# A sparse GAT kernel: empty list entries skipped by the gathers, their factor columns cleared on GpSimd, and two batches instead of one scaled on ScalarE

## The chip, the cores and the metric

The kernel runs on one core of one Trainium2 chip. The metric is the device time of one execution in microseconds (us); the number given for a kernel is the median of its runs. All data is float32 except where the code says otherwise.

## The reference

The input `x` is 8 batches x 2048 nodes x 128 features; `adj` is a 2048 x 2048 matrix of zeros and ones in which about 1 entry in 128 is set. Four graph layers follow each other: two attention layers with 8 heads and a small feed-forward network (layers 0 and 1), and two GAT layers (layers 2 and 3). The change is in the GAT layers. Each of them computes, cut to what matters:

```python
h = x @ W
s_i = h @ a_src
s_j = h @ a_dst
e = s_i[:, :, None] + s_j[:, None, :]
e = jnp.where(e >= 0, e, NEG_SLOPE * e)
e = jnp.where(adj[None, :, :] == 0, -jnp.inf, e)
att = jax.nn.softmax(e, axis=-1)
out = jnp.einsum('bij,bjd->bid', att, h)
y = out + x        # then a layer norm with ln_gamma, ln_beta
```

So each node takes a weighted mean over its neighbours' rows `h`. The weight of a neighbour is the exponential of a leaky relu of a sum of two numbers, one of the node and one of the neighbour.

## The kernel before

**Lists.** The kernel treats the graph as sparse. It sorts the 2048 nodes by degree into 16 blocks `t` of 128 nodes, one node per partition, and makes for each block a list of neighbour numbers of fixed length `CAPS[t]` (30 for the first block, 11 for the last; in the first, the last two list columns, called folded, hold the surplus of its 16 largest nodes). The lists of all blocks have 277 columns together. A node with fewer neighbours than its block's list has empty entries; they hold the number N = 2048, one past the last node.

**Tables and gathers.** For each layer `l` a table in DRAM has one row per node. In the attention layers a row is 8192 bytes (keys and values of 8 batches); in the GAT layers it is 4160 bytes: `h` of the 8 batches (8 x 128 numbers), and then 16 factors, two for each batch, which are the exponentials of the neighbour's number and of 0.2 times that number. `gather` (L319) issues one indirect DMA per list column on GpSimd's queue: it brings 128 rows, one into each partition. An entry over its `bounds_check` is skipped. In the attention layers entries over N - 1 are skipped. In the GAT layers the table has one row more, row N, which is all zeros, and entries up to N are fetched.

**Chunks.** In the GAT layers a chunk is up to 4 list columns of one block; there are 75 chunks in a layer. `fetch` takes the next of six buffers `kv` (`KVB = 6`) and issues the chunk's gathers, a few chunks ahead of the one in work. Each gather waits until TensorE has used up the old contents of its part of the buffer. `gat_chunk` then does, for a chunk:

- on VectorE, L785 multiplies the second factor of each batch by the node's own number, L786 takes the larger of the two factors (the weight, kept in `pair` in PSUM), and L791 does so once more for the last `SCALED` batches, into the small tile `ws` in SBUF;
- L797 on VectorE multiplies the rows of the first `8 - SCALED` batches by their weights; L802 on ScalarE multiplies those of the last `SCALED` batches, one instruction per list column and batch;
- in layer 2 alone, L808 on VectorE adds the rows of the chunk's last list column to those of its first;
- `add_up` (L326) on TensorE transposes and adds the chunk's rows into the accumulator `acc`, one matmul with the identity per list column and batch.

After a block's last chunk come its sums (L471 to L478), `outputs` (L678) and `gat_tail`: residual and layer norm on TensorE (L836) and ScalarE (L844, L852), a transpose (L859), and in layer 2 the projection for the next layer's table (L548, L557, L562 to L568), whose rows GpSimd scatters to DRAM (L515). In layer 3, L882 and L884 apply the norm's gain and offset and GpSimd scatters the block to the output (L886). SyncE loads and stores the blocks' states, one load per block and layer and one store.

**Order.** The order on each engine is the order in which the Python code emits the instructions, written out by hand in `layers` with generators: for chunk i it emits the weights and products of chunk i, then the pair sum and the adding up of chunk i - 1, and in between calls `slot`, which advances the tails by a step and lets `fetch` run. So on VectorE the L808 of a chunk comes after the L797 of the next, and on GpSimd gathers and scatters stand in one row.

A layer's first gathers can start once most rows of its table have been written; the lists of the first two blocks are sorted so that their first chunks need only the rows of early blocks.

Of the kernel before, what the change touches and what calls it, by code (L numbers as in the profile page):

```python
# [8 lines left out]
F32 = mybir.dt.float32  # L9
# [9 lines left out]
B, N, D = 8, 2048, 128  # L19
# [9 lines left out]
NB = 8  # L29
# [1 line left out]
LN_EXP = 6  # L31
KVB = 6
STATES = 4
SCALED = 1

# [47 lines left out]
def sparse_path(ctx: ExitStack, tc: tile.TileContext, ins: dict, out: bass.AP, flag: bass.AP):  # L85
# [10 lines left out]
    nc = tc.nc  # L96
# [3 lines left out]
    dram = ctx.enter_context(tc.tile_pool(name="dram", bufs=1, space=bass.MemoryType.DRAM))  # L100
# [39 lines left out]
    bufs = [const.tile([P, CHUNK], F32, name=f"kv{i}") for i in range(KVB)]  # L140
    turn = [-1]

    def buffer():
        turn[0] += 1
        return bufs[turn[0] % KVB]
# [155 lines left out]
    def width(l):  # L301
        return NB * (2 * D if l < 2 else D + 2)


    tables = [dram.tile([N + (l > 1), width(l)], F32, name=f"table{l}") for l in range(4)]

    x_rows = ins["x_nodes"]

# [9 lines left out]
    def gather(l, index, dst):  # L318
        nc.gpsimd.indirect_dma_start(  # L319
            out=dst, out_offset=None, in_=tables[l][:, :],  # L320
            in_offset=bass.IndirectOffsetOnAxis(ap=index, axis=0),
            bounds_check=N - (l < 2), oob_is_err=False,
        )

    def turn_into(dst, src, start):
        nc.tensor.matmul(  # L326
            dst, src, ident, start=start, stop=True, is_transpose=True, skip_group_check=True
        )
# [439 lines left out]
    def gat_chunk(l, c):  # L768
# [18 lines left out]
        if c["folded"]:  # L787
            box["wf"] = small.tile([P, FOLD, NB], F32, tag="wf", name="wf", bufs=1)
            nc.vector.tensor_max(box["wf"], wa, wb)
        ws = small.tile([P, 4, SCALED], F32, tag="ws", name="ws", bufs=3)  # L790
        nc.vector.tensor_max(  # L791
            ws[:, :ns, :], wa[:, :, NB - SCALED :], wb[:, :, NB - SCALED :]
        )
        yield
        hv = hs[:, :, : NB * D].rearrange("p s (b c) -> p s b c", b=NB)
        nv = NB - SCALED
        nc.vector.tensor_mul(  # L797
# [96 lines left out]
    def start():  # L894
# [173 lines left out]
        next(weights, None)  # L1068
        for i in (3, 4, 5):
            nc.scalar.copy(bufs[i], nil.to_broadcast([P, CHUNK]))  # L1070
        for l in (2, 3):
            nc.sync.dma_start(tables[l][N : N + 1, :], bufs[5][:1, : width(l)])


    def verdict():
# [29 lines left out]
    for l in range(4):  # L1105
        per = 2 if l < 2 else 4
        for t, k, ns, folded in pieces(l, per):
            c = dict(l=l, t=t, k=k, ns=ns, folded=folded, box=blocks[l][t])
# [11 lines left out]
    def fetch():  # L1120

        while now[1] < len(every):
            c = every[now[1]]
            l, t, k, ns = c["l"], c["t"], c["k"], c["ns"]

            if now[1] - now[0] > (4 if now[1] >= KVB and every[now[1] - KVB]["l"] > 1 else 3):
                return
            resorted = l > 0 and t < 2 and not c["folded"]
            need = NT - max([b for end, b in EARLY[t] if k + ns <= end] + [0] if resorted else [0])
            if put[l] < need:  # L1130
                return
            c["buf"] = buffer()[:, : ns * width(l)].rearrange("p (s c) -> p s c", s=ns)
            for i in range(ns):
                at = t * BASE if resorted else first[t]
                index = (sorted_lists if resorted else lists)[:, at + k + i : at + k + i + 1]
                gather(l, index, c["buf"][:, i])
            now[1] += 1
# [6 lines left out]
    def slot():  # L1144
        advance(threads)
        advance(tails)
        fetch()
        beat[0] += 1
        if beat[0] % 3 == 0 and hurry():
            advance(tails)  # L1150
# [40 lines left out]
    def layers():  # L1191
        threads.append(first_states((0,)))
        drain()
        fetch()
        begin(every[0])
        for _ in weights:
# [4 lines left out]
        for i in range(len(every) + 2):  # L1201
            c1, c, n1, n2 = (chunk(i + j) for j in range(-1, 3))
            while added:
                c2 = added.pop(0)
                go(c2)
                if c2["last"]:
                    threads.append(tail(c2["l"], c2["t"], c2["box"]))
            now[0] = i
            fetch()
            if c["k"] == 0:  # L1210
                l, t = c["l"], c["t"]
# [44 lines left out]
    with tc.manual_schedule():  # L1256
        nc.scalar.add_instruction(
            mybir.InstLoadActFuncSet(name=nc.get_next_instruction_name(), act_func_set_id=LN_EXP)
        )
        start()  # L1260
        layers()
# [521 lines left out]
```

## Time and profile before

| What | Value |
|---|---|
| Median of 3 runs | 3161.54 us (3149.05 to 3168.80) |
| Profiled execution, its own time | 3022.89 us |
| Span of the profiled execution | 3021.1 us |
| TensorE busy | 2517.4 us (83%) |
| TensorE weight loads busy | 2320.8 us (77%) |
| VectorE busy | 2743.3 us (91%) |
| ScalarE busy | 1379.7 us (46%) |
| GpSimd busy | 1784.3 us (59%) |
| Mean granted TensorE clock | 0.939 |
| Moved by DMA | 987.63 MB, mean 327 GB/s |

The page of the profile gives for each group of instructions its line, engine, operation, tiles (out<-in), count, busy time in us, mean duration in ns, and the idle time of its engine just before it with what ended that idle time. PE is TensorE, PEld its weight loads, DVE VectorE, ACT ScalarE, POOL GpSimd, SP SyncE. A table of stretches gives the busy time of each engine between two times, the granted clock, the mean busy share of the 16 DMA engines (values a little over 1 occur) and what they moved. The profiled execution is one of its own; the runs for the median were others.

### The profile page before, as it was taken

To read this page: it belongs to the slowest core of one execution; us is meant where nothing else is said; L and a number is where in the kernel's file an instruction comes from. 1 tells how busy PE (TensorE), PEld (TensorE's weight loads), DVE (VectorE), ACT (ScalarE), POOL (GpSimd) and SP (SyncE) were. 2 spreads that over 40 slices of the span, in tenths; PEclk is the share of its full clock that TensorE was granted. 3 is DMA by queue.
4 is the path that set the end of the run, shared out by engine and by line. 5 is a ranking of instruction groups with operands and counts; after the bars stand their busy time and mean duration, and the time that the engine had idled before them with its cause. 6 is when DMAs were issued, how large, how long until landed. Compare 5 with 4: busy or idle time off the path is not lost.

```text
span 3021.1 us, 52130 instructions
## 1 busy us (share of the span) xinstructions
PE 2517.4 (83%) x19258; PEld 2320.8 (77%) x19258; DVE 2743.3 (91%) x2945; ACT 1379.7 (46%) x4898; POOL 1784.3 (59%) x1293
## 2 busy tenths in 40 slices
PE   5756888789889999688888898999678898788886
PEld 3646777778788898677888788888578888687786
DVE  8788999999999998999999999998599998499996
ACT  4721333444445555043444454545345556244454
POOL 0057578677755644545546555554577775477773
PEclk8978999999999999899999999999798899899998
DMA  8688889988988887778888889886799999799995
GB/s 331 234 301 320 310 310 324 347 299 314 362 304 335 313 305 316 279 260 343 307 322 325 344 323 333 322 309 241 259 395 403 397 414 355 261 411 412 409 412 216
DMA packets 200692, 987.63 MB, mean 327 GB/s; under 512 B 31918, under 2 KB 33712, under 8 KB 128436
## 3 DMA queue, kind: packets, MB, share of 16 engines
q0 software_dynamic: 175024, 890.45, 77.7%
q1 hardware_dynamic: 20502, 75.52, 6.5%
q10 hardware_dynamic: 4904, 18.24, 1.9%
q8 instruction: 155, 2.54, 0.3%
q14 instruction: 107, 0.88, 0.1%
HBM read 937.16 MB, written 91.55 MB: 341 GB/s over the span
## 4 chain that ended last, share of the span: by engine, by line
PE 36%; DVE 30%; DMA 16%; issue 9%; ACT 5%; POOL 1%; POOLq 0%; DVEq 0%; ACTq 0%
PE acc L326 12%; DMA kv<-table,lists 11%; DVE kv L640 9%; DVE kv L659 8%; PE pair L648 5%; DVE kv L645 4%; DMA kv<-table,sorted_lists 3%; PE m L752 3%; DVE kv L797 3%; PE m L731 2%; PE m L533 2%; PE m L333 2%; DMA table<-rows,perm 2%; PE m L557 1%; PE m L548 1%
## 5 line engine op out<-in xcount | busy, mean ns | idle before, releaser
L319 POOL DMA_INDIRECT kv<-table,lists x955 | 1334.0, 1397 | 764.8 <-PE acc L326 491.9
L326 PE MATMUL acc<-ident,kv 128*128 128x128 f32 x8208 | 1059.8, 285 | 180.0 <-DVE kv L659 98.4
L326 PEld LDWEIGHTS acc<-ident,kv 128*128 128x128 f32 x8208 | 978.2, 148 | 258.7 <-DVE kv L659 120.5
L640 DVE TENSOR_TENSOR kv<-kv,q 128x2048 f32<-128x2048 f32 (+1 forms) x282 | 629.2, 2231 | 46.5 <-DMA kv<-table,lists 18.7
L659 DVE TENSOR_TENSOR kv<-kv,w 128x2048 f32<-128x2048 f32 (+1 forms) x284 | 632.4, 2227 | 0.0
L648 PE MATMUL pair<-kv,ident 128*128 128x128 f32 (+1 forms) x3344 | 444.3, 284 | 141.5 <-issue 66.7
L797 DVE TENSOR_TENSOR kv<-kv,pair 128x3584 f32<-128x3584 f32 (+1 forms) x150 | 540.0, 3600 | 1.9
L648 PEld LDWEIGHTS pair<-kv,ident 128*128 128x128 f32 x3344 | 411.7, 197 | 167.1 <-issue 100.3
L653 ACT ACTIVATE w<-pair,lmask 128x64 f32<-128x64 f32 x554 | 144.7, 311 | 738.8 <-PE pair L648 738.7
L645 DVE TENSOR_TENSOR kv<-kv 128x1024 f32<-128x1024 f32 (+1 forms) x434 | 442.5, 1020 | 14.3
L494 ACT ACTIVATE n<-m,eps 128x128 f32<-128x128 f32 x512 | 181.5, 367 | 296.8 <-PE m L718 154.3
L319 POOL DMA_INDIRECT kv<-table,sorted_lists x153 | 188.4, 1231 | 126.3 <-PE acc L326 56.6
L802 ACT ACTIVATE kv<-kv,ws 128x128 f32<-128x128 f32 x554 | 177.9, 400 | 180.6 <-DVE ws L791 173.9
L844 ACT ACTIVATE n<-m,eps 128x128 f32<-128x128 f32 x256 | 90.8, 374 | 183.1 <-PE m L836 183.1
L515 POOL DMA_INDIRECT table<-rows,perm x57 | 85.1, 1493 | 132.9 <-ACT score L568 31.4
L752 PE MATMUL m<-w_L_w,hT 128*128 128x128 f32 x1024 | 156.2, 275 | 0.0
L501 ACT ACTIVATE n<-m,rs 128x128 f32<-128x128 f32 x512 | 146.3, 376 | 1.1
L752 PEld LDWEIGHTS m<-w_L_w,hT 128*128 128x128 f32 x1024 | 134.9, 192 | 0.0
L731 PE MATMUL m<-n1T,w_L_gnn_W 128*128 128x512 f32 x256 | 131.5, 597 | 0.6 <-ACT q L606 0.6
L333 PE MATMUL m<-ident,n 128*128 128x128 f32 x640 | 107.8, 291 | 11.9 <-ACT rows L562 7.5
L678 DVE TENSOR_TENSOR o<-acc,scale 128x512 f32<-128x512 f32 x128 | 82.9, 683 | 37.6 <-PE acc L326 23.3
L333 PEld LDWEIGHTS m<-ident,n 128*128 128x128 f32 x640 | 83.4, 151 | 36.2 <-issue 14.7
(238 smaller groups left out, 3615.4 us busy)
## 6 DMA issues: line engine op xcount, KB each, us to landing
kept<-xT SPq DMA_DIRECT2D x48, 512.0 KB, 6.2
xT<-kept SPq DMA_DIRECT2D x48, 512.0 KB, 7.5
kv<-in_adj_dram SPq DMA_DIRECT2D x16, 1024.0 KB, 6.5
table<-kv ACTq DMA_DIRECT2D x16, 1024.0 KB, 5.7
kv<-table,lists POOLq DMA_INDIRECT x955, 8.6
kv<-in_x_nodes_dram SPq DMA_DIRECT2D x16, 512.0 KB, 12.5
kv<-table,sorted_lists POOLq DMA_INDIRECT x153, 6.9
found<-cand POOLq DMA_DIRECT2D x16, 64.0 KB, 4.3
```

Source lines behind the costliest of these rows:

```text
L319: nc.gpsimd.indirect_dma_start(out=dst, out_offset=None, in_=tables[l][:, :], in_offset=bass.IndirectOffsetOnAxis(ap=index, axis=0), bound ...
L326: nc.tensor.matmul(dst, src, ident, start=start, stop=True, is_transpose=True, skip_group_check=True)
L333: nc.tensor.transpose(pt[:, j * P : (j + 1) * P], src[:, j, :], ident)
L494: nc.scalar.activation(dst[:, i, :], z[:, i, :], AF.Square, bias=eps, scale=D**-0.5, accum_out=ss[:, i : i + 1],)
L640: nc.vector.tensor_mul(kk, kk, q[:, None].to_broadcast([P, ns, NB, D]))
L645: nc.vector.tensor_add(kk[:, :, :, :width], kk[:, :, :, :width], kk[:, :, :, width : 2 * width])
L648: nc.tensor.matmul(sc, ident, kk[:, :, :, j : j + NH], start=j == 0, stop=j + NH == width)
L659: nc.vector.tensor_mul(vv, vv, w[:, k : k + ns, :].rearrange("p s (b h) -> p (s b) h", h=NH)[:, :, None, :] .to_broadcast([P, ns * NB, HD, ...
L731: nc.tensor.matmul(ph, wt["1"][:, f * P : (f + 1) * P], n1T.rearrange("p b c -> p (b c)"), start=True, stop=True,)
L752: nc.tensor.matmul(y[:, j, :], hT[:, f, j, :], wt["2"][:, f, :], start=False, stop=f == 1, skip_group_check=True,)
L797: nc.vector.tensor_mul(hv[:, :, :nv, :], hv[:, :, :nv, :], wc[:, :, :nv, None].to_broadcast([P, ns, nv, D]))
L802: nc.scalar.mul(hv[:, i, b, :], hv[:, i, b, :], ws[:, i, b - nv : b - nv + 1])
```

## The change

Three edits, all for the GAT layers:

- The tables lose their row of zeros, and the gathers of every layer skip entries over N - 1, so an empty entry leaves the old contents of its partition in the buffer.
- So that such an entry counts for nothing, `fetch` clears the 16 factor columns of all of the chunk's list columns with one GpSimd memset ahead of the chunk's gathers (128 partitions x up to 4 x 16 numbers); the weight of an entry that isn't fetched is then zero. The two loads of zero rows at the end of `start` go.
- `SCALED` goes from 1 to 2: L797 covers six batches instead of seven, L802 two instead of one, and `ws` is twice as wide.

```diff
-SCALED = 1
+SCALED = 2
...
-    tables = [dram.tile([N + (l > 1), width(l)], F32, name=f"table{l}") for l in range(4)]
+    tables = [dram.tile([N, width(l)], F32, name=f"table{l}") for l in range(4)]
...
         nc.gpsimd.indirect_dma_start(
             out=dst, out_offset=None, in_=tables[l][:, :],
             in_offset=bass.IndirectOffsetOnAxis(ap=index, axis=0),
-            bounds_check=N - (l < 2), oob_is_err=False,
+            bounds_check=N - 1, oob_is_err=False,
         )
...
-        for l in (2, 3):
-            nc.sync.dma_start(tables[l][N : N + 1, :], bufs[5][:1, : width(l)])
...
             c["buf"] = buffer()[:, : ns * width(l)].rearrange("p (s c) -> p s c", s=ns)
+            if l > 1:
+                nc.gpsimd.memset(c["buf"][:, :, NB * D :], 0.0)
             for i in range(ns):
```

In the changed kernel's order on GpSimd each memset stands directly ahead of its chunk's first gather, and that gather waits for the memset's semaphore besides those it waited for before.

## The prediction

> **What bounds the kernel now.** I read the page first, then the table of stretches, then the lines of GpSimd and VectorE in those stretches, and last the order of time on GpSimd alone. The change touches only the two GAT layers, so the averages over the span say little. From the starts of the score product (L785) the GAT layers run from 2078 us on; layer 3's first gather is issued at 2546 us and the last scatter at 3015 us. Each layer has 277 gathers of 128 rows in 75 chunks. I cut out the two steady parts, and the two parts in which a layer starts:
>
> ```profile
> core 0: us, PE busy (x) PEld busy (x) DVE busy (x) ACT busy (x) POOL busy (x), PEclk, DMA share, GB/s
> 2170.00:2525.00 355.00, 299.52 (x2297) 284.05 (x2297) 340.48 (x394) 190.84 (x761) 263.76 (x241) 0.90 1.01 397
> 2637.00:2975.00 338.00, 284.13 (x2331) 273.94 (x2330) 310.03 (x372) 164.09 (x638) 254.57 (x249) 0.93 1.02 410
> ...
> 2060.00:2170.00 110.00, 85.10 (x646) 76.58 (x645) 68.53 (x68) 54.03 (x209) 50.77 (x45) 0.89 0.65 228
> 2525.00:2637.00 112.00, 86.85 (x668) 83.62 (x668) 63.95 (x74) 47.02 (x191) 53.62 (x53) 0.85 0.76 286
> ```
>
> In both steady parts the DMA engines are full (1.01 and 1.02). VectorE is nearly full in layer 2 (340 of 355) and at 310 of 338 in layer 3. GpSimd seems to have a quarter free, but its busy time hides a fixed gap. The order of time on GpSimd, at the start of layer 3 where few transfers are under way:
>
> ```profile
> 2628.70 0.99 POOL L319 DMA_INDIRECT kv<-table,sorted_lists  x1 [0.30 <-issue]
> 2629.99 0.99 POOL L319 DMA_INDIRECT kv<-table,sorted_lists  x1 [0.30 <-DMA kv<-table,sorted_lists]
> 2631.29 0.99 POOL L319 DMA_INDIRECT kv<-table,sorted_lists  x1 [0.30 <-DMA kv<-table,sorted_lists]
> ```
>
> A gather is 0.99 us and then always 0.305 us until the next: 1.295 us at best. The previous transfer of the same lane had landed some 4 us earlier, so it isn't the DMA that sets this. GpSimd's floor in a stretch is its instructions times 1.295: 241 x 1.295 = 312 of 355 us in layer 2 and 248 x 1.295 = 321 of 338 us in layer 3. A gather also costs the DMA engines about the same: its 128 packets of 4160 bytes take 161 ns each by the median, eight on each of 16 engines, 1.29 us. So two resources stand at their limit side by side, and VectorE is a third in layer 2:
>
> ```profile
> L797 DVE TENSOR_TENSOR kv<-kv,pair 128x3584 f32<-128x3584 f32 (+1 forms) x63 | 226.2, 3590 | 0.9
> L808 DVE TENSOR_TENSOR kv<-kv 128x1024 f32<-128x1024 f32 x62 | 75.5, 1218 | 7.7 <-ACT kv L802 7.7
> L802 ACT ACTIVATE kv<-kv,ws 128x128 f32<-128x128 f32 x224 | 72.1, 401 | 25.0 <-DVE ws L791 18.2 <-issue 6.7
> L844 ACT ACTIVATE n<-m,eps 128x128 f32<-128x128 f32 x104 | 36.9, 375 | 96.3 <-PE m L836 96.3
> L902 POOL MEMSET kv<- x3: 141/141/141, 3.1 to 3.3; 128x64 f32 x3
> ```
>
> The reader should see that L797 is two thirds of VectorE's time, that ScalarE mostly waits for TensorE, and that a memset of 64 elements per partition is 141 ns.
>
> [...] for a layer-1 gather with 63 rows filled, eight of the 16 completions came within 1.8 us and the other eight 3.4 to 4.9 us after the first. [...] L802 lasts 401 ns, but four in a row take 1.28 us, 0.32 us each.
>
> **The change part by part.**
>
> Skipped entries. The inputs give 32733 edges for 277 x 128 = 35456 list slots, so 2723 entries (7.7%) per layer are empty. Layers 0 and 1 already skip: their gathers' 8192-byte packets number 65466 = 2 x 32733, so a skipped row moves nothing. The GAT layers now save 2 x 2723 packets. But nodes are sorted by degree within a block, so the empty rows lie in the high partitions. [...] With about 165 ns a packet that is 227 gathers x 1.32 x 0.044 = 13 us off layer 2's steady 355 us (floor 342), and 235 x 1.32 x 0.044 = 14 us off layer 3's 338 (floor 324). GpSimd's issue doesn't shrink: gathers with 96 or more empty entries in layers 0 and 1 have the same 0.99 us at their fastest.
>
> Memsets on GpSimd. 75 per layer, 62 and 64 in the steady parts. The built order puts each ahead of its chunk's gathers, and the first gather then also waits for the memset's semaphore. Behind it stand the chunk's other gathers, the row scatters (L515) or output scatters (L886) and the next chunks. Each memset breaks the 1.295 us rhythm by M = (end of the last gather to memset) + 0.14 + (memset's semaphore to gather) - 0.305. A gather held by TensorE's semaphore starts 0.259 us after it, over and over in the trace; a compute instruction behind another on GpSimd starts at once (the three memsets above start 0.08 us apart), but none stands behind a gather. Low end: 0 + 0.14 + 0.26 - 0.305 = 0.1 us. If the memset also has to sit out the 0.305: 0.4 us. High end: the semaphore counts like the landing of an old transfer, 0.745 us before the start: 0.05 + 0.14 + 0.745 - 0.305 = 0.63 us. A gain from it is excluded, since nothing is taken from GpSimd. I take 0.2 us, because the built program puts the memset's semaphore on the gather itself, as TensorE's is[...].
>
> One more batch on ScalarE. L797 goes from 3584 to 3072 elements; its two forms (3886 ns for 3584, 2953 for 2688) give 1.04 ns an element, so 0.53 us for a chunk of four, 0.49 on the mean: 62 x 0.49 = 30 us off VectorE in each steady part, 310 of 355 and 280 of 338 remain. ScalarE gets 224 more multiplications at 0.32 us, 72 us: 263 and about 239. The waits for TensorE (96 us in layer 2 alone) cover them; in a burst of tail work, where ScalarE is busy 12 us on end and TensorE waits for it, they would lengthen the burst by up to 4 us a block. VectorE's pair sum (L808) of a chunk comes after the next chunk's L797, so ScalarE has a chunk's time to finish.
>
> The two loads of a zero row on SyncE's queue at 162 us were 4 KB each with nothing behind them: nothing.
>
> Sum against the profiled execution's 3022.9 us (span 3021.1). Layer 2: DMA 342, GpSimd 312 + 62 x 0.2 = 324, VectorE 310, TensorE 300; with 2 us of friction (my guess) 344, that is 11 us less. Layer 3: DMA 324, GpSimd 321 + 64 x 0.2 = 334, plus 2: 336, that is 2 us less; here GpSimd takes over from the DMA engines. The two starts have 24 of the 150 chunks, some of whose memsets are on the way: 2 us more; ScalarE's longer bursts: 2 us more. Together 9 us less, 0.30%. The runs' median of 3161.5 us lies 139 us above the profiled execution, for a reason that the profile doesn't show; I carry the share over: 3161.5 x 0.9970 = 3152.
>
> **The rivals.**
>
> Slower: the hand-over on GpSimd costs 0.63 us. Layer 3 becomes 321 + 64 x 0.63 + 2 = 363, 25 more; layer 2 312 + 39 + 2 = 353, 2 less; the starts 8 more, ScalarE 2 more. 33 us more, 1.1%: 3196. It speaks for it that GpSimd is already at 95% of its floor in layer 3 and that every chunk passes through it; against it the 0.259 us after TensorE's semaphore. The point from which it decides is M = 0.4 us: there 64 x 0.4 - 15 = 11 us lost in layer 3 meet layer 2's gain.
>
> Faster: the memset fits the gap (M = 0.05) and the packets, now fewer, also lose their stretch from 161 to 165 ns. Layer 2: 21 less, layer 3: 14 less (GpSimd's floor 324 holds it there): 35 us, 3125. Against it: it needs both.
>
> ScalarE's bursts eat layer 2's gain: TensorE waits 10 us there for L859 already. Layer 2 unchanged, the rest as forecast, and its gain of 11 gone: 2 us more, 3164, within 1%.
>
> The change doesn't do what it says: skipped rows still cost their packets. Then only the memsets' price is left, about 13 us in layer 3 and 2 in the starts: 3177. The count in layers 0 and 1 speaks against it.
>
> **How the numbers follow.** Forecast 0.5; slower rival 0.2; faster 0.12; ScalarE 0.15; no skip 0.03. A change of 1% (32 us) is about what a measurement of this kernel can tell from none. The forecast's own spread (M of 0.1 to 0.4) gives 3144 to 3169. The range takes in the faster rival's and the slower one's centre, and some scatter between runs: 3118 to 3200. Faster by over 1%: 0.12 and a little of the forecast, 0.15. Slower by over 1%: the slower rival and a little of ScalarE's case, 0.23. Within: 0.62.
>
> **What would show it.** Right: packets of 4160 bytes fall from 75776 to 70330; the gap from a chunk's last gather to the next chunk's first is about 0.5 us with a memset in it, against 0.305; the DMA share falls below 1.0 in layer 3 while GpSimd's gathers stand in an unbroken row; VectorE's L797 is near 3.1 us; layer 2 shrinks more than layer 3. Wrong: a gap of 0.9 us or more around each memset, ScalarE as the releaser of TensorE's L326 or VectorE's L808 in most chunks, or a DMA share still at 1.02.

## The result, and the profile after

The change made the kernel slightly slower: 3183.9 us (median of 7 runs, 3162.88 to 3189.59) against 3164.42 us (3149.05 to 3174.81), a ratio of 1.0058 with a 95% interval of 1.0032 to 1.0084. A second set of runs (e8, on the chip called B below) gave 1.0104 (1.0077 to 1.013). The forecast was a small gain, 9 us; by the medians the loss is 19 us in the first set and 26 us in the second, whose ratio makes it 33 us.

One thing is needed before the profiles can be read. The runs of this study were made on several chips of the type, and they are not alike. On four of them the kernel before takes 3146 to 3161 us at a mean granted clock of 0.921 to 0.922; on the fifth it takes 3031.66 us at 0.939. The profiled execution on which the prediction was worked out (3022.89 us, clock 0.939) looks like the fifth; the timed runs look like the other four, and all experiments but e17 and e18 come from them. Each chip was used for one series of runs, so whether the chip itself makes the difference, or something about that series, isn't shown. I call the chips A to E; the table gives the kernel before on each.

| Chip | Experiments | Kernel before, median | Mean clock |
|---|---|---|---|
| A | e1 to e4 | 3147.71 us | 0.922 |
| B | e5 to e8 | 3150.17 us | 0.921 |
| C | e9c to e12c | 3160.86 us | 0.921 |
| D | e13 to e16 | 3146.25 us | 0.921 |
| E | e17, e18 | 3031.66 us | 0.939 |

So the profile after must be set beside a profile of the kernel before from an ordinary chip (e1, chip A, span 3143.4 us), not beside the first one. Table of stretches, the change (first gather of layer 2 at 2070 us, of layer 3 at 2620 us, span 3161.1 us):

```profile
2170.00:2600.00 430.00, 330.83 (x2302) 306.26 (x2302) 316.30 (x399) 251.97 (x971) 282.85 (x317) 0.81 0.88 317
2700.00:3100.00 400.00, 309.52 (x2253) 280.82 (x2251) 275.72 (x364) 219.09 (x829) 268.34 (x319) 0.87 0.92 329
```

The same stretches of the kernel before on chip A (layer 3 from 2611 us):

```profile
2170.00:2600.00 430.00, 337.00 (x2367) 314.56 (x2367) 352.66 (x407) 198.00 (x779) 281.71 (x258) 0.83 0.94 350
2700.00:3100.00 400.00, 319.06 (x2370) 293.78 (x2370) 315.32 (x375) 165.54 (x651) 259.16 (x252) 0.87 0.96 357
```

The columns are those of the prediction: TensorE, its weight loads, VectorE, ScalarE and GpSimd busy, then clock, DMA share and GB/s. Already before the change nothing is as full here as in the first profile: DMA 0.94 and 0.96 in place of 1.01 and 1.02, VectorE 353 of 430 us, TensorE at a clock of 0.83. The change takes load from VectorE (353 to 316) and from the DMA engines, puts 54 us on ScalarE in each stretch, and TensorE gets fewer matmuls done in the same time (2302 for 2367). The groups on the page after show that each edit did what it says:

```profile
L797 DVE TENSOR_TENSOR kv<-kv,pair 128x3072 f32<-128x3072 f32 (+1 forms) x150 | 466.3, 3108 | 1.7
...
L802 ACT ACTIVATE kv<-kv,ws 128x128 f32<-128x128 f32 x1108 | 337.3, 400 | 53.7 <-DVE ws L791 22.4
...
L808 DVE TENSOR_TENSOR kv<-kv 128x1024 f32<-128x1024 f32 x75 | 91.7, 1223 | 98.4 <-ACT kv L802 78.0
```

L797 fell from 540.0 us on the page before to 466.3, 0.49 us a chunk, and L802 nearly doubled, from 177.9 to 337.3. The last line has the new wait: VectorE stood idle 78 us before its pair sum, until ScalarE's product was done; in the stretch of layer 2 shown with the prediction that was 7.7 us. In the waits of layer 2 (2170 to 2600 us; us in total, times, longest), the change:

```profile
DVE kv L808 <- ACT kv L802: 68.6, 20, 9.7
...
POOL kv L319 <- PE acc L326: 58.5, 19, 8.3
```

and the kernel before on chip A:

```profile
POOL kv L319 <- PE acc L326: 69.6, 29, 8.0
...
DVE kv L808 <- ACT kv L802: 45.8, 13, 8.9
```

On chip A the kernel before already had 45.8 us of this wait. A sign of what a batch on ScalarE costs could be seen there, but not in the profile that I had.

### The profile page after: what moved, and what is told of

Its sections match the earlier page's. It is cut to its first block, busy times and chain, and to the rows that moved or that the text cites. A ratio compares the mean times of both kernels' runs of the same rounds, so it can differ in the third digit from the quotient of the medians.

```text
span 3161.1 us, 52991 instructions
## 1 busy us (share of the span) xinstructions
PE 2585.7 (82%) x19258; PEld 2358.4 (75%) x19258; DVE 2673.6 (85%) x2945; ACT 1537.2 (49%) x5452; POOL 1778.9 (56%) x1443
## 2 busy tenths in 40 slices
DMA packets 200694, 965.03 MB, mean 305 GB/s; under 512 B 37362, under 2 KB 39156, under 8 KB 128432
## 4 chain that ended last, share of the span: by engine, by line
PE 42%; DVE 24%; issue 10%; DMA 9%; ACT 8%; POOL 3%; another core or an unknown queue 1%; POOLq 0%; ACTq 0%; DVEq 0%
PE acc L326 17%; DVE kv L640 8%; DVE kv L659 8%; DMA kv<-table,lists 7%; PE pair L648 5%; DVE kv L645 4%; PE m L731 2%; PE m L752 2%; POOL kv L319 2%; ACT kv L802 2%; ACT n L844 2%; PE m L333 2%; PE m L533 2%; PE m L836 2%; PE m L557 2%
## 5 line engine op out<-in xcount | busy, mean ns | idle before, releaser
L326 PE MATMUL acc<-ident,kv 128*128 128x128 f32 x8208 | 1089.1, 287 | 212.6 <-DVE kv L659 95.2
L326 PEld LDWEIGHTS acc<-ident,kv 128*128 128x128 f32 x8208 | 988.9, 149 | 309.7 <-issue 147.1
L797 DVE TENSOR_TENSOR kv<-kv,pair 128x3072 f32<-128x3072 f32 (+1 forms) x150 | 466.3, 3108 | 1.7
L802 ACT ACTIVATE kv<-kv,ws 128x128 f32<-128x128 f32 x1108 | 337.3, 400 | 53.7 <-DVE ws L791 22.4
L844 ACT ACTIVATE n<-m,eps 128x128 f32<-128x128 f32 x256 | 90.5, 369 | 251.2 <-PE acc L326 150.0
L808 DVE TENSOR_TENSOR kv<-kv 128x1024 f32<-128x1024 f32 x75 | 91.7, 1223 | 98.4 <-ACT kv L802 78.0
L333 PE MATMUL m<-ident,n 128*128 128x128 f32 x640 | 116.4, 304 | 24.1 <-ACT kv L802 8.9
```

Source lines behind the costliest of these rows:

```text
L326: nc.tensor.matmul(dst, src, ident, start=start, stop=True, is_transpose=True, skip_group_check=True)
L333: nc.tensor.transpose(pt[:, j * P : (j + 1) * P], src[:, j, :], ident)
L797: nc.vector.tensor_mul(hv[:, :, :nv, :], hv[:, :, :nv, :], wc[:, :, :nv, None].to_broadcast([P, ns, nv, D]))
L802: nc.scalar.mul(hv[:, i, b, :], hv[:, i, b, :], ws[:, i, b - nv : b - nv + 1])
```

## The experiments

The first eight ask which edit costs the time, the next four why ScalarE's batch costs it and what sets layer 3, the last six why fewer packets gave nothing. Ratios are to the kernel before on the same chip, with 95% intervals; microseconds given for an experiment are its ratio's distance from 1 times the median of before on that chip.

**e1, the kernel before again.** No edit.

> The kernel before, unchanged, for a second profile of it. If the profiled execution of 3022.9 us was unusual (theory U), this profile shows a span near 3150 us, with the GAT layers 100 us or more longer than the 944 us of the first profile and gaps in TensorE's rows that wait for nothing shown. If the profile is usual and only the timed runs are longer (rival), the span is again near 3020 us and the GAT layers near 944 us.

1.0016 (0.9998 to 1.0033). Its profile (3143.4 us) isn't like the first one. Layers 0 and 1 last the same in both, 950 us each; the GAT layers last 539 and 533 us instead of 480 and 475.

**e2, skipping and memset, one batch on ScalarE.** The change with `SCALED = 1`.

> The changed kernel with SCALED back at 1: skipped entries and memsets alone. Theory S (the second batch on ScalarE is what costs: the pair sum and TensorE's adding up wait for it): faster than before by 5 to 20 us, 3145 to 3160. Theory G (the memset in GpSimd's row costs more than the skipped packets give): slower than before by 5 to 20 us, and about as slow as the whole change, 3170 to 3185.

0.9999 (0.9975 to 1.0022). Two of the three edits together move nothing beyond the interval, some 8 us either way. Neither theory had foreseen that.

**e3, two batches alone.**

```diff
-SCALED = 1
+SCALED = 2
```

> The kernel before with SCALED at 2 alone: row N still fetched, no memsets. Theory S: slower than before by 20 to 40 us, 3185 to 3205, with L808 and TensorE waiting for L802 as in the profile after. Theory G: no slower than before, 3150 to 3165, since VectorE loses 0.5 us a chunk.

1.0125 (1.008 to 1.0169): the whole loss is here.

**e4, the memset alone.** The memset in `fetch`, on rows that are all fetched.

> The kernel before with the memset ahead of each GAT chunk's gathers added, nothing else: row N still fetched, SCALED 1. It measures the memset by itself. By the profile after, a memset adds 0.14 us to GpSimd's row, 150 times, 21 us at most. Theory S: 0 to 15 us slower than before. Theory G: 20 us slower or more.

1.0001 (0.9981 to 1.0021). 150 memsets on GpSimd cost nothing beyond the interval, some 7 us either way.

**e5 and e6, two batches in one layer.**

```diff
-SCALED = 1
+SCALED_OF = {2: 2, 3: 1}
...
+        SCALED = SCALED_OF[l]
```

(e6: `{2: 1, 3: 2}`.)

> The kernel before with two batches on ScalarE in layer 2 alone (layer 3 keeps one; no skipping, no memsets). Theory S1 (the loss is layer 2's, where VectorE's pair sum L808 waits for ScalarE's products): 25 to 45 us slower than before, as much as two batches in both layers (38 us). Theory S2 (ScalarE's longer row delays the tails in both layers): about half of that, 15 to 22 us slower.

> The kernel before with two batches on ScalarE in layer 3 alone, which has no pair sum. Theory S1: within 8 us of before, on either side. Theory S2: 15 to 22 us slower.

e5 1.0078 (1.0054 to 1.0102), e6 1.0005 (0.998 to 1.003). Within these intervals the loss is in layer 2 alone, 24.6 us at chip B's level. Nor does VectorE's relief of half a microsecond a chunk gain anything in layer 3 that they show.

**e7, VectorE's pair sum without ScalarE's batches.** `SCALED = 2`, but L808 adds only the six batches that VectorE multiplied, and TensorE adds the other two of the last column itself, so L808 waits for no one.

```diff
-            nc.vector.tensor_add(hv[:, :pairs], hv[:, :pairs], hv[:, left:ns])
+            nc.vector.tensor_add(hv[:, :pairs, :nv], hv[:, :pairs, :nv], hv[:, left:ns, :nv])
...
+        for i in range(left, ns):
+            for b in range(nv, NB):
...
+                    turn_into(acc[:, b, :], hv[:, i, b, :], False)
```

> Two batches on ScalarE in both layers, no skipping, no memsets; layer 2's pair sum on VectorE covers only the six batches that VectorE scaled itself, and TensorE adds the other two batches of the last list column with two matmuls of its own (0.2 us a chunk). Theory S1: the loss of 38 us goes; within 10 us of before. Theory S2, or TensorE's own wait for ScalarE as the cause: still 25 us slower or more.

1.0134 (1.01 to 1.0168), against 1.0104 for the change on the same chip. The most visible new wait, L808's, is gone (0.0 us of idle time before L808), and the loss stays. But VectorE now waits elsewhere in layer 2 (2170 to 2650 us):

```profile
DVE o L678 <- PE acc L326: 72.5, 8, 11.3
DVE o L678 <- ACT kv L802: 41.8, 4, 14.4
DVE ws L791 <- ACT kv L802: 19.2, 12, 2.9
```

In e3 the first two of these were 9.0 and 5.3 us, and the third isn't among VectorE's waits there. The edit also gives TensorE two matmuls more a chunk: in the steady part of layer 2, from the 51st gather to the last, it was busy 361 us, against 336 in e3. So e7 shows that taking this one wait away gains nothing; it doesn't show that the wait is harmless.

**e8, the change again.**

> The changed kernel once more, beside the others on the same chip. If skipping gives back part of what the second batch costs, it is 15 to 25 us slower than before, and some 15 to 20 us faster than two batches alone (38 us slower). If the two only differed by chance between chips, it is 30 to 40 us slower.

1.0104 (1.0077 to 1.013), 33 us. That speaks for chance between chips as the difference between the change and e3; the interval, 24 to 41 us, leaves room for a small part given back by skipping.

**e9c, less TensorE work in layer 3.** Two of the eight batches of every list column but a block's first are not added up (522 of 2216 matmuls left out).

```diff
...
-            for b in range(NB):
+            for b in range(NB - (less if k + i > 0 else 0)):
...
```

> The kernel before, in whose layer 3 TensorE leaves out two of the eight batches' adding up in every list column but a block's first (522 of the layer's 2216 such matmuls; those two batches of the output are then not sums). Everything else stays. Theory P (in the ordinary executions TensorE alone sets layer 3's time, so that fewer packets, memsets and VectorE's 0.5 us a chunk count for nothing there): 45 to 80 us faster than before. Rival (the gathers set it, by DMA or by GpSimd's rhythm): less than 10 us faster.

0.9984 (0.9966 to 1.0001): 5 us, at most 11, though TensorE is, just ahead of VectorE, the busiest engine of that layer (319 and 315 of 400 us in e1's table). Theory P falls.

**e10c, idle work on ScalarE.** One batch on ScalarE as before; in layer 2 each list column gets one more multiplication (277 in all) from constants into a tile that nobody reads.

```diff
...
+        for i in range(ns if l == 2 else 0):
+            nc.scalar.mul(idle, ident, node[:, i : i + 1])
```

> The kernel before with, in layer 2, one more multiplication of 128x128 on ScalarE per list column, behind L802, on a tile that nobody reads: 277 x 0.32 = 89 us of ScalarE's row and nothing that another engine waits for. Theory O (what the second batch costs is room in ScalarE's row: the tails' steps behind it come late, and TensorE waits for them in order): 20 to 40 us slower. Theory D (the cost is that TensorE and the pair sum wait for the second batch's products): within 8 us of before.

1.0046 (1.0023 to 1.0068), 14.5 us. Nothing waits for this work's result, VectorE isn't relieved, and no transfer changes; only the place in ScalarE's row is taken. It costs more than half of the 24.6 us of the real second batch. Behind this work the one real batch comes later too: the pair sum's wait for it in layer 2 is 70.5 us, against 45.8 in e1. So e10c shows that the place costs, and not which of ScalarE's late results does the harm.

**e11c, no batch on ScalarE in layer 2.** VectorE multiplies all eight there; L791 and L802 go from layer 2.

```diff
-SCALED = 1
+SCALED_OF = {2: 0, 3: 1}
...
+        if SCALED > 0:
...
```

> The kernel before with no batch on ScalarE in layer 2 (L797 covers all eight there; layer 3 keeps one). Theory O: the mirror image of the loss as long as VectorE has room, 10 to 25 us faster. If VectorE's row becomes layer 2's bound (0.5 us more a chunk on 321 of 380 us): slower by up to 15 us.

0.9935 (0.9918 to 0.9951), 3139.03 against 3160.86 us: faster than both kernels. VectorE is fuller in this version's layer 2 than in e1's:

```profile
2170.00:2600.00 430.00, 336.17 (x2424) 312.85 (x2425) 386.69 (x353) 133.80 (x563) 292.65 (x262) 0.84 0.96 357
```

VectorE is busy 387 of 430 us (353 in e1), and still more gets done than before (2424 matmuls in the stretch for 2367, 262 instructions on GpSimd for 258).

**e12c, layer 3's pair sum moved to VectorE.** Two batches on ScalarE in layer 3 (one in layer 2), and L808 in every second chunk of it, which takes matmuls from TensorE.

```diff
...
-        pairs = min(ns // 2, 1) if l == 2 else 0
+        pairs = min(ns // 2, 1) if l == 2 or k // 4 % 2 == 0 else 0
```

> A version that follows from theory P: one batch on ScalarE in layer 2 and two in layer 3, and layer 3 also adds a chunk's last list column to its first on VectorE, in every other chunk (41 of 75), which takes 41 x 8 matmuls off TensorE and puts 41 x 1.2 us on VectorE. Theory P: 25 to 45 us faster than before. Rival: no faster than before.

1.0048 (1.0029 to 1.0066): the room that the second batch gives on VectorE in layer 3 can't be turned into time this way.

**e13, three quarters of the rows in layer 3.** On e2's version (which is level with before):

```diff
-            bounds_check=N - 1, oob_is_err=False,
+            bounds_check=(3 * N // 4 if l == 3 else N) - 1, oob_is_err=False,
```

> Skipping and memset with one batch on ScalarE, and in layer 3 the gathers also skip every node number of 1536 and over: a quarter of the neighbours are left out, 25% of layer 3's packets go, and every instruction on GpSimd, VectorE, ScalarE and TensorE stays. Without the last edit this version measured 0.9999. Theory D (the DMA engines, with their slow packets, set layer 3 in ordinary executions): a quarter of some 316 us of packet time goes, and the layer shrinks until the next row decides (GpSimd's gathers at 320 us of 381): 30 to 60 us faster, 0.98 to 0.99. Theory G (GpSimd's own issue row): within 5 us, since every gather is still issued. Theory T (TensorE with its throttle, or a pause that no other engine ends): within 5 us.

0.997 (0.9948 to 0.9991), 9 us. Three times as many further packets as the change skips (25% of 32733 against 2723) give less than a third of the least that theory D asked. The at most 5 us of theories G and T lie within the interval. The stretch in layer 3:

```profile
2700.00:3000.00 300.00, 236.59 (x1736) 217.53 (x1736) 229.74 (x270) 115.19 (x450) 199.41 (x237) 0.86 0.77 259
```

The DMA share is down to 0.77 and the stretch holds no more work for it: e2 has 1714 matmuls and 236 instructions on GpSimd in its 2700 to 3000 us, at a DMA share of 0.92.

**e14, fewer gathers in layer 3.** On e2's version, the last column of each chunk of three or four isn't gathered.

```diff
-            for i in range(ns):
+            for i in range(ns - (l == 3 and ns > 2)):
```

> Skipping and memset with one batch on ScalarE, and in layer 3 the last list column of each chunk of three or four is not gathered at all (74 of 277 gathers; its factors are cleared by the memset, so a part of the neighbours is left out); the work on VectorE, ScalarE and TensorE stays. Both GpSimd's row (74 x 1.295 = 96 us) and the packets (about 27%) fall. Theory D: like the kernel with three quarters of the rows, 0.98 to 0.99. Theory G: 30 to 60 us faster, 0.98 to 0.99, while the kernel with three quarters of the rows stays within 5 us. Theory T: within 5 us, as the other.

0.9705 (0.9672 to 0.9738), 93 us. Layer 3 lasts 448 us instead of some 530, and VectorE becomes its bound:

```profile
2690.00:2990.00 300.00, 266.00 (x2229) 255.43 (x2228) 286.93 (x342) 155.53 (x608) 189.25 (x234) 0.95 0.93 327
```

That is the direction of theory G, though it had asked for 30 to 60 us only; but the clock in that stretch also rose to 0.95 from 0.84 (e2, same stretch), and the columns that are not gathered reach TensorE as zeros, so the gain could come from what TensorE is given. e17 and e18 are for that.

**e15, no batch on ScalarE in either layer.** e11c with `{2: 0, 3: 0}`.

> The kernel before with no batch on ScalarE in either GAT layer: VectorE multiplies all eight batches, L791 and L802 go. In layer 2 alone this measured 0.9935. In layer 3 a second batch moved nothing (1.0005). If ScalarE's row costs nothing in layer 3 and VectorE has room (it was busy 303 of 380 us in an ordinary execution; 64 more products of 0.5 us make 335), the result is that of layer 2 alone, 0.993 to 0.995. If VectorE becomes layer 3's bound with its load, 10 to 20 us are lost again: 0.997 to 1.000.

0.9892 (0.9858 to 0.9926), 3118.96 against 3146.25 us: better than I expected of it, and the fastest version here that computes all of the reference. VectorE has the room in layer 3. Whether the layer gains by it too isn't settled: e11c's interval, on chip C, overlaps with this one.

**e16, no batch in layer 2, with skipping and memset.**

> No batch on ScalarE in layer 2, one in layer 3, with the change's skipping and memset. If the packets that are skipped cost nothing there even when ScalarE is out of the way, the result is that of no batch in layer 2 alone, 0.993 to 0.994. If ScalarE's row had hidden the gain of fewer packets in layer 2, a part of the 13 us reckoned for it shows now: 0.989 to 0.992.

0.9922 (0.9896 to 0.9948), in agreement with e11c's 0.9935. So ScalarE hadn't hidden a gain of the skipped packets: even with its row free in layer 2 they give none that the intervals show.

**e17 and e18, issues and zeros told apart, on chip E.** e17: e14's columns are gathered, but with a bound that skips their rows (issue kept, packets gone, zeros kept). e18: as e14, and TensorE adds the chunk's first column a second time in place of the last (issue gone, packets gone, no zeros).

```diff
...
+                gather(l, index, c["buf"][:, i], 0 if l == 3 and ns > 2 and i == ns - 1 else N - 1)
```

```diff
...
-                    turn_into(acc[:, b, :], rows[:, i, b, :], k + i == 0 and b % 4 == 0)
+                    turn_into(acc[:, b, :], rows[:, 0 if again and i == n - 1 else i, b, :], k + i == 0 and b % 4 == 0)
```

> As the kernel with fewer gathers in layer 3 (0.9705), but the last column's gather of each chunk of three or four is issued and then skips its rows (all but those of node 0; these neighbours are left out again). GpSimd's row is whole again, while the packets stay about 27% fewer and TensorE still gets zeros for 74 columns. Theory G (GpSimd's issue row: 74 x 1.295 = 96 us): the gain is gone, 0.99 to 1.00. Theory Z (the gain came from the zeros, which TensorE does at a less throttled clock: it was 0.96 there against 0.88): 0.97 to 0.975, as without the issue.

> As the kernel with fewer gathers in layer 3 (0.9705), but TensorE adds the chunk's first column a second time in place of the last, which is not gathered: the matmuls are as many and none of them is of a column of zeros; VectorE and ScalarE do what they did (the last column's neighbours are left out and the first's count twice). Theory G: the gain stays, 0.97 to 0.975. Theory Z: the gain goes, 0.99 to 1.00. If a part goes, both have a share.

e17 0.9951 (0.9934 to 0.9969), e18 0.9863 (0.9842 to 0.9883): 15 and 42 us against the kernel before; their layers 3 last 462 and 440 us, 475 in the first profile. (e2's version wasn't run on chip E, so skipping and memset have a share in both that isn't known.) Table of stretches, e17:

```profile
2637.00:2975.00 338.00, 287.36 (x2388) 277.07 (x2385) 312.41 (x368) 170.36 (x669) 257.02 (x305) 0.94 0.89 300
```

and e18:

```profile
2645.00:2945.00 300.00, 264.96 (x2246) 256.60 (x2245) 295.42 (x355) 159.17 (x625) 189.48 (x234) 0.95 0.91 331
```

e17 can be laid beside the first profile of before, over the same stretch: the DMA share is down from 1.02 to 0.89, and the gathers from the 51st to the last take the same 325 us. GpSimd's row accounts for it: 237 gathers and scatters at 1.295 us and 61 memsets at 0.14 make 315 of these 325 us. Without the issues (e18) the layer shortens until VectorE is full, 295 of 300 us. So on chip E theory G holds for the larger part of the gain, 27 of 42 us, and zeros don't explain it: e18 has none. For the rest of e14's 93 us on chip D they can't be excluded, since what chip D loses there isn't lost on chip E to begin with (see the pauses below).

## Why the prediction was right or wrong

**Right: what the edits do.** The bytes moved fell from 987.63 to 965.03 MB, and the packets of 4160 bytes from 75778 to 70330: 2 x 2723 rows and the two loads of zero rows. Before:

```profile
DMA packets 200692, 987.63 MB, mean 327 GB/s; under 512 B 31918, under 2 KB 33712, under 8 KB 128436
```

After:

```profile
DMA packets 200694, 965.03 MB, mean 305 GB/s; under 512 B 37362, under 2 KB 39156, under 8 KB 128432
```

The number of packets didn't fall: 5444 became small ones. In the trace a skipped row is a packet of 4 bytes that takes 9 ns; "moves nothing" was right enough. L797's new mean is 3.11 us, as reckoned.

**Right: the price of a memset, M.** In order of time on GpSimd, the change, layer 3 (start, us, line, and idle time before it):

```profile
2841.59 1.02 POOL L886 DMA_INDIRECT out_dram<-n,perm  x1 [0.30 <-issue]
2842.62 0.17 POOL L1133 MEMSET kv<- 128x64 f32 x1
2843.06 1.02 POOL L319 DMA_INDIRECT kv<-table,lists  x1 [0.27 <-issue]
```

From the scatter's end at 2842.61 to the gather at 2843.06 are 0.44 to 0.45 us where 0.305 stood: M = 0.14 us, taken as 0.2 with 0.1 to 0.4 as its range. Of the 150 hand-overs in this profile 93 take less than 0.5 us, 0.44 by the median. The memset starts at once (0.00 us after the instruction ahead of it, by the median of the 93), the gather 0.27 us after it, as a gather after TensorE's semaphore does (0.26). A memset beside VectorE's pair sum takes no longer in this profile: the 13 that ran beside an L808 took 0.16 to 0.18 us, the 137 others 0.14 to 0.18, both 0.166 by the median. The slower rival (0.63) is out. Even this small price doesn't show in the runs (e4).

**Wrong: ScalarE's second batch, 2 us.** This is the term that failed. The prediction set 72 us of new work against 96 us in which ScalarE waited for TensorE, allowed up to 4 us more per block in a burst, and then put down 2 us in all. Its own upper end, 4 us for each of the 13 blocks of the steady part (104 L844, eight a block), is 52 us; the measured cost is 25 us (e5). Two of its reasons failed as well. "ScalarE has a chunk's time to finish" did not hold: L808 waited 78 us for L802. And TensorE's wait for L859 was not 10 but 20 us already in the first profile: 10.4 before L548, which is the prediction's 10, and 9.2 before L326.

ScalarE's free time isn't where its work is. In e1 ScalarE is busy 198 of 430 us of layer 2, and still the 277 multiplications of e10c, which nobody reads, cost 14.5 us. As I read the traces, a block's tail goes to and fro between TensorE and ScalarE (L836, L844, L852, L859, L548 and on), each tail step stands in ScalarE's row behind the eight multiplications of a chunk (eight in a row take 2.45 us by the median of the profile after, four took 1.28 in the first profile), and TensorE waits at the tail's next step with the adding up of chunks behind it.

In the steady part of layer 2, TensorE's idle time that ends with ScalarE is 22 to 26 us without a batch (23.8 in e11c), 30 to 48 with one on chips A to D (36.6 in e1, 48.0 in e9c), 47 to 51 with two, and 63.8 with the idle work (e10c). Single executions scatter, and the ranges of one batch and two touch, so the medians must carry it, and they do: none, one and two batches in layer 2 cost -21, 0 and +25 us.

Not all of the loss is idle time. The steady layer 2 with none (e11c), one (e1) and two batches (e5):

```profile
2202.00:2592.00 390.00, 315.61 (x2296) 293.35 (x2297) 358.45 (x326) 129.91 (x544) 267.28 (x238) 0.86 0.97 360
...
2197.00:2601.00 404.00, 324.82 (x2308) 302.90 (x2309) 333.43 (x389) 193.99 (x769) 261.51 (x239) 0.84 0.94 349
...
2201.00:2631.00 430.00, 333.95 (x2288) 308.62 (x2286) 303.71 (x380) 255.37 (x984) 258.54 (x238) 0.81 0.89 327
```

From e1 to e5 the part grows by 26 us. TensorE's idle time grows by 17 of them; for the other 9 it is busy longer with as many matmuls, at a granted clock of 0.81 instead of 0.84.

That ScalarE's place in the row matters is shown by e10c. By which of its late results the delay is passed on is read from the traces and not shown. Most of TensorE's idle time above ends with steps of the tails: in e5 34 of 47 us with the steps that are L852 and L859 in the kernel before, and 5 with L802. But in the profile after L802 ends 17.7 us of it, and VectorE's idle time that ends with ScalarE grows with the batches too: 0, 47 to 76 and 75 to 100 us with none, one and two (61 in e7, 84 in e10c). e7 moved a part of that wait and did not end it. The 10 us by which the real batch exceeds the idle work are not explained and may be chance: the intervals, 17 to 32 and 7 to 21 us, overlap.

The rival "ScalarE's bursts eat layer 2's gain" had this mechanism, but let it go only as far as there was a gain to eat.

**Wrong: layer 2's 11 us and layer 3's 2 us.** The steps "DMA floor 342" and "GpSimd 334" assumed that the resources which were full in the one profile set the time of the runs. The 0.044 in the first of them, by how much less the fullest DMA engine would have to carry, was my estimate besides: no trace here shows which engine carries which row. On chips A to D those resources don't set it: e2, which has the two edits that these steps price, gains nothing (0.9999). Steady layer 3 of e1 takes 375 us. In it the gathered rows take 326 us of each DMA engine's time (363 with all other packets), and GpSimd's row takes 307 us at 1.295 us an instruction. With skipping (e2) the rows' time falls to 316, less than in proportion, since the mean packet goes from 179 to 185 ns (the median stays at 161; the slowest one in a hundred take 690 and 840 ns); the part takes 381 us. That the DMA engines don't set it is shown by e13, where their share fell to 0.77 and the part still took 377 us. What differs from the first profile is TensorE. In e1, in order of time, layer 3:

```profile
2796.89 0.60 PE L326 MATMUL acc<-ident,kv 128*128 128x128 f32 x4 [0.87 <-issue]
2798.34 0.27 PE L326 MATMUL acc<-ident,kv 128*128 128x128 f32 x1 [0.85 <-issue]
2799.05 0.27 PE L326 MATMUL acc<-ident,kv 128*128 128x128 f32 x1 [0.44 <-issue]
2799.78 0.46 PE L326 MATMUL acc<-ident,kv 128*128 128x128 f32 x1 [0.46 <-issue]
2800.49 0.46 PE L326 MATMUL acc<-ident,kv 128*128 128x128 f32 x1 [0.25 <-issue]
2801.20 3.01 PE L326 MATMUL acc<-ident,kv 128*128 128x128 f32 x13 [0.26 <-issue]
```

Single matmuls come 0.7 us apart and wait for nothing that the profile shows; a row of 13 takes 3.01 us right after. Idle time of this kind sums to 52.6 us before L326 between 2700 and 3100 us in e1; the first profile, e17 and e18 have none. Of 37 such steps of 0.65 to 0.75 us between the starts of two matmuls of L326 in e1's GAT layers, 19 lie within 2 us of a point where the granted clock drops to half, where even spreading would put 6. Half clock covers 314 us of these layers in e1, 193 in the first profile. Whether a pause brings the drop or follows it isn't shown. In the two GAT layers the half-clock stretches last 3.4, 6.8, 10.2 or 13.7 us in 33 of 35 cases in the first profile and in 39 of 42 in the change's. With time lost there, it fits that on chips A to D a packet less or a microsecond less on VectorE is worth nothing. What causes the pauses stays open: fewer matmuls (e9c) don't remove the lost time, fewer gathers with zeros in their place (e14) remove most of it (TensorE's idle time without a wait that the profile shows is 14 us in steady layer 3, against 63 in e1), and the runs that tell those apart (e17, e18) fell on chip E, whose profiles show none there.

On chip E itself, e17 and e18 run layer 2 with skipping, memset and one batch: 477 us in both, 480 in the first profile. VectorE was idle for only 14 of the 349 steady us there, which leaves little of the forecast 11 us to gain without VectorE's relief. The full change wasn't run on chip E; whether it gains there is open.

**Wrong: the 139 us.** The prediction saw that its profile lay 139 us under the runs' median and carried the percentage over. That gap was the warning that the profile showed another balance than the runs.

## What to carry to other kernels

An engine with idle time on the average is not free (e10c: 14.5 us for work that nobody reads, on an engine that e1 shows busy 198 of 430 us): count what stands directly ahead of the steps that another engine waits for, per burst, and multiply by the bursts before you write down a small number. If the profiled execution is some per cent off the timed runs, take a second profile of the unchanged kernel before you price anything by what is full in the first. To learn whether transfers or their issue set a stage, take away packets without issues (a tighter bound) and then issues as well.

## What was not expected of the hardware

- Series of runs on chips of one type differ by 4% on this kernel (3031.66 against 3146 to 3161 us), nearly all of it in the two GAT layers (955 us in the first profile, 1072 in e1's); the attention layers take about 950 us each on both kinds.
- A row skipped by the gather's bound is a packet of 4 bytes and 9 ns, and a gather whose rows are nearly all skipped still holds GpSimd as long as a full one (e17: 990 ns by the median for both).
- With fewer packets the rest get slower on the mean, not faster: 179, 185 and 197 ns for all, 92% and three quarters of the rows of layer 3 (e1, e2, e13), with the median at 161 ns in each. The number of rows isn't all of it: with about as many rows (20800 and 19400 in the steady part) e17 has 196 ns and e18 184; between e17's lie 12200 packets of 4 bytes, between e18's 2900.
- In the profile of e1 TensorE starts matmuls 0.65 to 0.75 us apart with no wait in the profile, 19 of 37 times within 2 us of a drop of its clock to half. The idle time before L326 for which layer 3 shows no wait is 52.6 us in e1 (chip A, 2700 to 3100 us), 43.8 in e9c (chip C, 2750 to 3090) and 39.7 in e13 (chip D, 2700 to 3100); the first profile and those on chip E (e17, e18) have none of it there.
